# One product of every second block moved from POOL to DVE, and one diagonal of every second pair of groups from POOL to ACT, in a state space layer

## The chip, the cores and the metric

The kernel runs on one core of one Trainium2 chip. The metric is the device time of one execution in microseconds (us). The engines are called PE (matrix products), DVE (vector), ACT (scalar and activation functions), POOL (GpSimd) and SP (which only issues transfers here). SBUF is the memory that all of them work on; PSUM is the small memory into which PE writes.

## The reference

Four layers are applied to x of shape 8 x 512 x 256: three transformer blocks with conditioning, and then a bidirectional state space layer with a gated MLP. Only the last layer is touched. Cut to what matters:

```python
def _mamba(h, ...):                       # h: (8, 512, 256)
    x, z = jnp.split(h @ in_proj_W, 2, axis=-1)        # 512 channels each
    x = silu(causal_conv(x, conv_w) + conv_b)
    xdbl = x @ x_proj_W
    dt = softplus(xdbl[..., :16] @ dt_proj_W + dt_proj_b)
    Bm, Cm = xdbl[..., 16:48], xdbl[..., 48:]          # 32 states
    A = -exp(A_log)
    def step(hst, inp):
        dA = exp(dt_t[:, :, None] * A)
        hst = hst * dA + dt_t[:, :, None] * B_t[:, None, :] * x_t[:, :, None]
        return hst, einsum('bdn,bn->bd', hst, C_t)
    y = scan(step, ...) + Dp * x
    return y * silu(z) @ out_proj_W
...
x = x + g1 * (_mamba(h) + flip(_mamba(flip(h))))       # then norm, gated MLP, residual
```

## The kernel before

The first three layers come first and are left as they are. The state space layer then runs 16 **steps**, one for each of the 8 batch rows b and each direction, forward before reversed. I number them from 0, so even steps are forward and odd steps reversed. All five engines execute in the order in which the program was written (a schedule kept by hand), so an instruction that waits holds up everything behind it on its engine.

A step works on 512 channels in 4 blocks c of 128 and on 32 states in 8 groups of 4, taken as 4 pairs of groups gp. `recur` has 64 iterations k, with c = k // 16, gp = k % 16 // 4 and j = k % 4 (32 channels). For each k:

- `fill` (line 1372): PE multiplies the transposed u times dt (`ut`, one tile per block c) with diagonal matrices `dg` that hold B, and so lays dt * B * x for 128 pairs of channel and state out in PSUM (`bx`, 3 buffers).
- `decay` (line 1347): ACT makes exp(dt * A) in two activations (`da`, `N_DA` = 3 tiles).
- `scan` (line 1386): DVE runs two recurrences of 128 x 512; it is issued two iterations after `fill`. After every second k POOL multiplies four results at once by C (line 1390, `hs` times `cs`).
- `sums` (lines 1411 to 1418): after every four k PE adds over the states into `yc`.

While a step runs, `prep3` prepares the next one. It is a generator that is advanced once for each even k, if the budget `credit` allows: convolution, projections, softplus for `dt`, and last `transposed(c)` for the four blocks. `transposed(c)` first multiplies u by dt into `uc` (line 1132, on POOL), lets two turns pass (`N_UC_LATE`), has PE transpose `uc` in four pieces into a PSUM bank (line 1140) and has ACT copy that to `ut` (line 1145). Block c + 1 starts two turns after block c (`STAGGER`). There is one buffer for `uc` (`N_UC` = 1) and one PSUM bank for all products outside the recurrence; a stream takes it with `free_bank` and gives it up with `taken`. During forward steps from batch row 1 on, the MLP of the batch row before (`project`, `mlp3`) shares that bank: its last products are read by DVE at line 1205. What is left of `prep3` and of the MLP at the end of a step is issued before the next step starts:

```python
            live = [(prep, 0), (post, 1)]
            while any(n == 0 for _, n in live):
```

`diagonal` makes `dg` of the next step for one pair of groups gp and one quarter s of the time axis, in the last block of a step and the beginning of the next:

```python
                    if c == 3 and nxt:
                        for s in range(4):
                            later(1 + 3 * s, lambda gp=gp, s=s: diagonal(nxt, gp, s))
```

A letter for each s says on which engine: "A" is 8 activations of 128 x 64 on ACT (line 1320), "P" is one product of 128 x 512 on POOL and "V" the same on DVE (line 1324). `DIAG` = "AAPA" gives s = 2 to POOL for every gp. The very first pair of groups of step 0 has letters of its own.

Of the kernel before, what the change touches and what calls it, by code (L numbers as in the profile page):

```python
# [10 lines left out]
ALU = mybir.AluOpType  # L11
# [14 lines left out]
N_U, N_UT, N_UC, N_DT, N_HS = 7, 5, 1, 5, 4  # L26
N_DA, AHEAD, SPREAD = 3, 0, (6, 13, 14, 15)
N_UC_LATE = 2
SUMS_LATE, DIAG, STAGGER, RATE, CREDIT = 3, "AAPA", 2, 4.0, 4.0


C_ID, C_MEAN, C_EM, C_E32, C_E64 = 0, 128, 256, 384, 896
# [42 lines left out]
def dit_mamba_kernel(ctx: ExitStack, tc: tile.TileContext, t, out):  # L75
    nc = tc.nc
# [43 lines left out]
    with ExitStack() as actx:  # L120
# [725 lines left out]
        with tc.manual_schedule(  # L846
# [13 lines left out]
            for l, cfg in enumerate(CFGS):  # L860
                us = [u for u in units if u.cfg is cfg]
# [10 lines left out]
    with ExitStack() as mctx:  # L872
# [108 lines left out]
        def free_bank():  # L981

            me = now[0]
            while held[0] or (want[1 - me] and last[0] == me):
                want[me] = True
                yield WAIT
            want[me] = False
            held[0], last[0] = True, me
            return bank()

        def taken():
            held[0] = False
# [26 lines left out]
        def halves(v):  # L1019

            return v.rearrange("p (r s t) -> p s r t", r=2, s=4)
# [36 lines left out]
        def prep3(b, rev):  # L1058
# [16 lines left out]
            us = st.pop("us")  # L1075
# [34 lines left out]
            dt = mp_.tile([128, 4, L], F32, tag="dt", name="dt")  # L1110
# [18 lines left out]
            def transposed(c):  # L1129

                uc = mp_.tile([128, 4, 2, 64], F32, tag="uc", name="uc", bufs=N_UC)
                nc.gpsimd.tensor_tensor(uc, halves(us[c]), halves(dt[:, c, :]), ALU.mult)
                for _ in range(N_UC_LATE):
                    yield 0
                while n_ut[0] - n_ut[1] >= N_UT:
                    yield WAIT
                n_ut[0] += 1
                p = yield from free_bank()
                for s in range(4):
                    nc.tensor.transpose(  # L1140
                        p[:, 128 * s : 128 * s + 128], uc[:, s].rearrange("p r t -> p (r t)"), ident
                    )
                yield 1
                ut = mp_.tile([128, 4, 128], F32, tag="ut", name="ut", bufs=N_UT)
                nc.scalar.copy(ut.rearrange("p s d -> p (s d)"), p)
                taken()
                uts.append(ut)
                yield 0

            live, c, i = [], 0, 0  # L1150
            while live or c < 4:
                if i % STAGGER == 0 and c < 4:
                    live.append(transposed(c))
                    c += 1
                cost = 0
                for g in list(live):
                    n = next(g, None)
                    while n == WAIT:
                        yield WAIT
                        n = next(g, None)  # L1160
                    if n is None:
                        live.remove(g)
                    cost += n or 0
                i += 1
                yield cost + LAST
# [144 lines left out]
        def diagonal(step, gp, s, on=None):  # L1310

            if s == 0:
                dg[step, gp] = mp_.tile([128, 4, 4, 64, 2], F32, tag="dg", name="dg", bufs=n_p)
            o = dg[step, gp][:, s]
            bt = st[("bt",) + step][:, s, 8 * gp : 8 * gp + 8]
            on = on or DIAG[s]
            if on == "A":
                for i in range(2):
                    for n in range(4):
                        nc.scalar.activation(  # L1320
                            o[:, n, :, i], eye, AF.Copy, scale=bt[:, 4 * i + n : 4 * i + n + 1]
                        )
            else:
                (nc.vector if on == "V" else nc.gpsimd).tensor_tensor(
                    o, eye[:, None, :, None].to_broadcast([128, 4, 64, 2]),
                    bt.rearrange("p (i n) -> p n i", i=2)[:, :, None, :].to_broadcast([128, 4, 64, 2]),
                    ALU.mult,
                )
# [22 lines left out]
        def recur(step, nxt, ys):  # L1351
# [75 lines left out]
            for k in range(n_k):  # L1427
                c, gp, j = k // 16, k % 16 // 4, k % 4
                run_due(1)
                if k % 2 == 0:  # L1430
                    fill(k)
                    fill(k + 1)
                    for i in range(0 if k else -AHEAD, 2):
                        decay(step, nxt, k + AHEAD + i)
                n_ut[1] += k % 16 == 15
                later(2, lambda k=k: scan(k))
                if j == 3:
                    later(2 + SUMS_LATE, lambda c=c, gp=gp: sums(c, gp))
# [3 lines that stand above are left out]
                        later(4, lambda gp=gp: spread_c(nxt, gp))  # L1442
                if k % 16 in SPREAD:
                    i = SPREAD.index(k % 16)
                    if c < 3:
                        spread(step, 4 * (c + 1) + i)
                    elif nxt and ("dt",) + nxt in st:
                        spread(nxt, i)
                if not nxt and c == 3 and j == 3 and gp < 3:

                    w = mp_.tile([128, 4, 4, 64, 2], F32, tag="dg", name="dg", bufs=n_p)
                    w = w.rearrange("p s n t i -> p (s n t i)")[:, 0:1024]
                    fetch(("w_g1", "w_g2", "w_g3")[gp], w=w)
                yield k
# [44 lines left out]
        for gp in range(n_p):  # L1499
            spread_c(steps[0], gp)  # L1500
            for s in range(4):
                if gp == 0:
                    diagonal(steps[0], gp, s, "VAVA"[s])
                else:
                    later(4 * gp - 3 + s // 2, lambda gp=gp, s=s: diagonal(steps[0], gp, s))
# [154 lines left out]
```

## Time and profile before

| | |
|---|---|
| Median of 3 runs | 6146.75 us (6141.36 to 6157.84) |
| The profiled execution, its own time | 6153.84 us |
| Span of that profile | 6151.9 us |
| Mean granted TensorE clock | 0.962 |
| Scans, DVE, line 1386 | 2048, mean 1198 ns |
| Products by C, POOL, line 1390 | 512, mean 4569 ns |
| Decays, ACT, line 1347 | 2048, mean 716 ns |
| Fills, PE, line 1372 | 65536 matmuls, 1120.5 us busy |
| Diagonals, ACT, line 1320 | 1528, mean 343 ns |
| Diagonals, POOL, line 1324 | 63, median 1232 ns |
| u times dt, POOL, line 1132 | 64, median 1285 ns |

Times in the profile are microseconds from the start of the span. A row of the timeline reads: start, length, engine, line, operation, tile written and tiles read, shapes, count of merged instructions, and in brackets the idle time before it and what ended it. Instructions of one engine overlap at their ends, so the length of a merged row divided by its count is the pace, and the mean of one is longer. The state space layer takes the span from about 3382 us on.

### The profile page before, as it was taken

The page shows a single profiled execution, that of the slowest core. Times are in us where ns is not written, and L with a number is a line of the kernel's source. Part 1 is how long each engine was busy: PE and PEld are TensorE (multiplying, and loading weights), DVE is VectorE, ACT ScalarE, POOL GpSimd, SP SyncE. Part 2 cuts the span into 40 slices and gives each one's busy share as a digit, 9 for nine tenths or more (in the row PEclk, how much of TensorE's full clock was granted, in tenths as well). Part 3 has the DMA queues.
Part 4 walks back from the last instruction along what each step waited for, and adds up shares of the span by engine and source line. Part 5 has one row for each costly group of instructions (what it writes and reads, how often), then busy time and mean ns, then how long its engine had stood idle before and what let it go on. Part 6 is the DMA issues. An engine that isn't in the chain of part 4 may idle for free. (4 is left out here: it accounts for less than half of the span.)

```text
span 6151.9 us, 221688 instructions
## 1 busy us (share of the span) xinstructions
PE 5588.1 (91%) x99484; PEld 2771.0 (45%) x99484; DVE 4131.2 (67%) x5157; ACT 3556.9 (58%) x6876; POOL 3162.6 (51%) x1419
## 2 busy tenths in 40 slices
PE   8999999999999989899997889898888989888887
PEld 4333334555555543333332445444544545444544
DVE  4554545655656554455541898888888898888987
ACT  2444444444444443344543777777787777777784
POOL 2011002323222231111000899999899999899997
PEclk8999999999999999899998999999999999999999
DMA  2010102332333321110100211222121211222120
GB/s 90 23 27 23 31 22 77 115 89 82 93 88 91 89 79 29 39 27 21 28 14 22 72 55 53 66 58 66 54 67 55 60 55 52 63 61 66 52 67 26
DMA packets 338211, 345.60 MB, mean 56 GB/s; under 512 B 50016, under 2 KB 240480, under 8 KB 337264
## 3 DMA queue, kind: packets, MB, share of 16 engines
q1 hardware_dynamic: 196944, 262.70, 14.8%
q10 hardware_dynamic: 140320, 68.72, 3.9%
q8 instruction: 784, 12.85, 0.9%
q14 instruction: 163, 1.34, 0.1%
HBM read 253.63 MB, written 51.38 MB: 50 GB/s over the span
## 5 line engine op out<-in xcount | busy, mean ns | idle before, releaser
L1386 DVE TENSOR_TENSOR_SCAN hs<-da,bx 128x512 f32<-128x512 f32 x2048 | 2304.4, 1198 | 216.0 <-PE bx L1372 124.2
L1390 POOL TENSOR_TENSOR hs<-hs,cs 128x2048 f32<-128x2048 f32 x512 | 2324.5, 4569 | 216.4 <-DVE hs L1386 139.1
L1347 ACT ACTIVATE da<-dtr,negA 128x512 f32<-128x512 f32 x2048 | 1393.8, 716 | 492.7 <-DVE hs L1386 482.0
L1372 PE MATMUL bx<-dg,ut 64*32 64x128 f32 x65536 | 1120.5, 273 | 194.7 <-DVE hs L1386 100.3
L1372 PEld LDWEIGHTS bx<-dg,ut 64*32 64x32 f32 x65536 | 929.4, 106 | 611.4 <-issue 472.7
L685 DVE TENSOR_REDUCE aux<-s 128x1 f32<-128x512 f32 x1024 | 638.3, 684 | 617.0 <-PE s L680 616.8
L587 POOL TENSOR_SCALAR pr<-pr,sums 128x512 f32<-128x512 f32 x512 | 361.5, 724 | 906.7 <-DVE sums L585 906.7
L736 ACT ACTIVATE pt<-s 128x512 f32<-128x512 f32 x1024 | 528.0, 602 | 468.2 <-PE s L730 467.9
L1418 PE MATMUL yc<-hs,r 128*32 128x512 f32 x4096 | 565.4, 618 | 37.5 <-POOL hs L1390 35.8
L577 ACT ACTIVATE pr<-s,negm 128x512 f32<-128x512 f32 x512 | 345.4, 686 | 249.7 <-DVE negm L576 237.5
L680 PE MATMUL s<-kT,qT 32*128 32x512 f32 x2048 | 374.8, 662 | 63.1 <-ACT pt L736 25.0
L767 PE MATMUL s<-g,w_w 128*128 128x512 f32 x768 | 368.1, 630 | 34.3 <-ACT g L832 34.3
L576 DVE TENSOR_REDUCE negm<-s 128x1 f32<-128x512 f32 x512 | 317.6, 683 | 108.4 <-PE s L566 108.4
L793 POOL COPY aux<-rec 128x1024 f32<-128x1024 f32 x16 | 16.6, 1036 | 718.0 <-DVE rec L791 718.0
L1320 ACT ACTIVATE dg<-eye,bt 128x64 f32<-128x64 f32 x1528 | 381.6, 343 | 0.8 <-PE bx L1372 0.7
L730 PE MATMUL s<-work,kT 32*128 32x512 f32 x2048 | 370.8, 656 | 2.9 <-DVE work L694 2.9
L416 PE MATMUL s<-h,wqkv 128*128 128x512 f32 x768 | 362.3, 611 | 10.1 <-POOL h L403 6.6
L416 PE MATMUL s<-h,w_w 128*128 128x512 f32 x768 | 356.8, 606 | 8.5 <-POOL h L403 8.5
L384 POOL TENSOR_TENSOR xs<-x 128x512 f32<-128x512 f32 x32 | 40.6, 1269 | 622.3 <-DMA x<-x_mid 210.3
L1418 PEld LDWEIGHTS yc<-hs,r 128*32 128x32 f32 x4096 | 120.4, 111 | 384.5 <-issue 268.6
L700 PE MATMUL s<-pt,vt 128*32 128x512 f32 x2048 | 279.9, 617 | 1.3 <-ACT ot L707 1.3
L767 PEld LDWEIGHTS s<-g,w_w 128*128 128x128 f32 x768 | 150.0, 202 | 232.6 <-issue 169.5
(202 smaller groups left out, 6576.8 us busy)
## 6 DMA issues: line engine op xcount, KB each, us to landing
dtr<-dt_s SPq DMA_DIRECT2D x1024, 64.0 KB
qT<-v_dram ACTq DMA_DIRECT2D x256, 128.0 KB
kT<-v_dram ACTq DMA_DIRECT2D x256, 128.0 KB
cs<-c_s SPq DMA_DIRECT2D x256, 128.0 KB
wqkv<-in_wqkv_dram SPq DMA_DIRECT2D x98, 256.0 KB
v_dram<-vt SPq DMA_DIRECT2D x32, 512.0 KB
dt_s<-dt SPq DMA_DIRECT2D x15, 1024.0 KB
x_mid<-x SPq DMA_DIRECT2D x24, 512.0 KB
```

Source lines behind the costliest of these rows:

```text
L416: nc.tensor.matmul(p, w[:, k, o : o + 128], src[:, k, :], start=k == 0, stop=k == n - 1)
L680: nc.tensor.matmul(ss[j], u.qT[r, c, qt * 128 : (qt + 1) * 128], u.kT[r, c, :], start=True, stop=True)
L685: nc.vector.tensor_reduce(negp[c % 2][:, qt, i : i + 1], ss[j], AX.X, ALU.max, negate=True)
L730: nc.tensor.matmul(ss[j], u.kT[r, c, i * 128 : (i + 1) * 128], q2[u, c][r, :], start=True, stop=True)
L736: nc.scalar.activation(pt[j // 2][:, j % 2, :], ss[j], AF.Exp)
L767: nc.tensor.matmul(p, w[:, first + c, m * 128 : (m + 1) * 128], srcs[c], start=c == 0, stop=c == n - 1)
L1320: nc.scalar.activation(o[:, n, :, i], eye, AF.Copy, scale=bt[:, 4 * i + n : 4 * i + n + 1])
L1347: nc.scalar.activation(da[:, i, :], dtr[step, 4 * c + j], AF.Exp, scale=negA[:, 4 * c + j, g : g + 1])
L1372: nc.tensor.matmul(bx[k][32 * n : 32 * n + 32, r, 128 * s : 128 * s + 128], uts[c][64 * r : 64 * r + 64, s, 32 * j : 32 * j + 32], d[64 * ...
L1386: nc.vector.tensor_tensor_scan(h, back(da[:, i, :]), back(x[:, i, :]), 0.0, ALU.mult, ALU.add)
L1390: nc.gpsimd.tensor_tensor(hs[t_], hs[t_], cs[step, k % 16 // 4][:, None, :, :].to_broadcast([128, 2, 2, L]), ALU.mult,)
L1418: nc.tensor.matmul(yc[c][32 * j : 32 * j + 32, :], r32, h[j // 2][:, j % 2, i, :], start=False, stop=gp == n_p - 1 and i == 1, tile_positi ...
```

## The change

In `transposed`, u times dt of blocks 1 and 3 is computed by DVE and that of blocks 0 and 2 by POOL as before. In `diagonal`, the letters depend on gp: for gp 0 and 2 they stay "AAPA", for gp 1 and 3 they are "AAAA".

```diff
-SUMS_LATE, DIAG, STAGGER, RATE, CREDIT = 3, "AAPA", 2, 4.0, 4.0
+SUMS_LATE, DIAG, STAGGER, RATE, CREDIT = 3, ("AAPA", "AAAA"), 2, 4.0, 4.0
...
             def transposed(c):
 
                 uc = mp_.tile([128, 4, 2, 64], F32, tag="uc", name="uc", bufs=N_UC)
-                nc.gpsimd.tensor_tensor(uc, halves(us[c]), halves(dt[:, c, :]), ALU.mult)
+                (nc.vector if c % 2 else nc.gpsimd).tensor_tensor(uc, halves(us[c]), halves(dt[:, c, :]), ALU.mult)
...
             o = dg[step, gp][:, s]
             bt = st[("bt",) + step][:, s, 8 * gp : 8 * gp + 8]
-            on = on or DIAG[s]
+            on = on or DIAG[gp % 2][s]
```

## The prediction

> **What bounds the kernel now.** I read the page's busy shares first, then the waits, then the timeline engine by engine where one step of the state space layer hands over to the next.
>
> ```profile
> PE 5588.1 (91%) x99484; PEld 2771.0 (45%) x99484; DVE 4131.2 (67%) x5157; ACT 3556.9 (58%) x6876; POOL 3162.6 (51%) x1419
> ```
>
> These are averages over four layers. In the window 3570 to 3940 us, inside the state space layer, POOL is busy 344.7 of 370 us, DVE 329.5, PE 326.6 and ACT 291.5, so four engines have little slack and order decides. I call two iterations of k a pair: 4 scans on DVE, 4 decays on ACT, one 4.57 us product on POOL. Inside a step pairs start every 4.44 to 4.5 us and POOL starts 0.2 to 0.5 us behind the scans that feed it: DVE paces POOL there. The excess lies at the handover, which I call a seam. From the start of every 128th scan, steps 2 to 14 last 176.1 us if forward and 167.0 us if reversed, of which one gap of 12.2 us (forward) or 7.5 us (reversed) beyond a normal pair is the seam.
>
> The seam after a reversed step (step 3), PE, POOL and ACT:
>
> ```profile
> 4056.16 0.90 PE L1140 MATMUL bank<-base,uc 128*128 128x128 f32 x4
> 4062.25 1.11 PE L1140 MATMUL bank<-base,uc 128*128 128x128 f32 x4 [5.19 <-POOL uc L1132]
> 4063.29 3.58 PE L1418 MATMUL yc<-hs,r 128*32 128x512 f32 x16
> ...
> 4059.75 1.23 POOL L1324 TENSOR_TENSOR dg<-eye,bt 128x512 f32<-128x512 f32 x1
> 4060.92 1.28 POOL L1132 TENSOR_TENSOR uc<-u,dt 128x512 f32<-128x512 f32 x1
> ...
> 4051.69 2.03 ACT L1320 ACTIVATE dg<-eye,bt 128x64 f32<-128x64 f32 x8
> 4053.61 2.56 ACT L1347 ACTIVATE da<-dtr,negA 128x512 f32<-128x512 f32 x4
> 4056.06 2.02 ACT L1320 ACTIVATE dg<-eye,bt 128x64 f32<-128x64 f32 x8
> 4057.97 0.57 ACT L1145 COPY ut<-bank 128x512 f32<-128x512 f32 x1
> 4063.40 0.59 ACT L1145 COPY ut<-bank 128x512 f32<-128x512 f32 x1 [4.86 <-PE bank L1140]
> ```
>
> PE waits 5.19 us for the fourth product uc, which stands behind POOL's queue. That is what the change attacks, in 7 seams. But ACT has no idle time from 4028.9 to 4058.5, and the copy of the third transpose ends at 4058.5, only 3.7 us before the fourth transpose starts; that transpose needs the one PSUM bank the copy empties.
>
> The seam after a forward step (step 4):
>
> ```profile
> 4223.84 2.02 ACT L1320 ACTIVATE dg<-eye,bt 128x64 f32<-128x64 f32 x8
> 4225.76 2.55 ACT L1347 ACTIVATE da<-dtr,negA 128x512 f32<-128x512 f32 x4
> 4228.21 2.01 ACT L1320 ACTIVATE dg<-eye,bt 128x64 f32<-128x64 f32 x8
> 4230.12 0.56 ACT L1145 COPY ut<-bank 128x512 f32<-128x512 f32 x1
> ...
> 4230.74 4.41 PE L973 MATMUL bank<-g,w 128*128 128x512 f32 x6 [2.49 <-ACT ut L1145]
> ```
>
> Here PE waits not for POOL but for ACT: after the copy, products and transposes go through the one bank in turn until 4241.8, so whatever delays the copy at 4230.12 delays the next step.
>
> **What moves.** 32 of the 64 products uc go from POOL (1.285 us) to DVE. The nearest DVE rows, additions and products of two SBUF tiles of 128x512 (L384, L1324), take 0.69: DVE gains 32 x 0.69 = 22 us. 32 of POOL's 63 diagonals (1.232) become 8 ACT activations each; 16 stand in 3.92 us, so 1.96 per diagonal and 63 us on ACT. POOL loses 32 x 1.285 + 32 x 1.232 = 80.5 us. PE and SP keep their order. None of these totals is the answer; the positions are.
>
> **The new wait.** uc has one buffer. Product c = 1 is now on DVE and may only write once PE has transposed c = 0, and c = 3 once c = 2 is transposed. POOL ran late enough for this to cost little (8.5 us in all). DVE is early: in the built order uc1 stands mid-pair, and DVE reaches it at 4034.65 in step 3 while the transposes of c = 0 end at 4036.53, 1.9 us later (1.9 to 3.4 over the seven reversed steps); uc3 is reached 1.9 to 4.6 us before its transposes end. In forward steps uc1 comes 1.7 to 1.9 us early. Behind a waiting uc stand all scans, and ACT's decays behind those, since three da tiles let ACT run one pair and a half ahead.
>
> Can DVE run uc beside a POOL product? One row bounds it:
>
> ```profile
> 2267.37 2.49 DVE L756 SCALAR_TENSOR_TENSOR x<-y,modT,x 128x512 f32<-128x512 f32 x1 [3.11 <-ACT y L754]
> ...
> 2266.96 2.36 POOL L401 TENSOR_TENSOR h<-h,rstd 128x1024 f32<-128x1024 f32 x1
> ```
>
> The DVE operation, whose large inputs both lie in SBUF, took 2.49 us instead of 0.75 and ended 0.54 us after POOL's at 2269.32. So uc on DVE costs 0.69 if it runs freely and up to 4.57 + 0.69 = 5.26 if it is held from the start of a product. The rows nearest in form give 0.69 and the sum below would be 44; the one row beside a long POOL product gives the remainder of that product and the sum is 52 (reversed seams 1.2 us longer each). I take the second, because POOL is busy 93% of this layer. The Trainium skill, "SBUF — State Buffer", section "Who interferes with whom", has a rule that speaks against this change: a DVE instruction with two SBUF inputs and a GpSimd instruction that reads SBUF exclude each other for the whole instruction, whichever started first, while one SBUF input does not contend. By the rule every uc on DVE pays the remainder and the sum is 52; the scans, one input in PSUM, would stay as they are.
>
> **Reversed seam, walked through** (step 3; half a pair of scans 2.25, a decay pair 1.25, from 4 in 2.55). DVE waits for the transposes until 4036.6; the POOL product begun at 4033.5 ends at 4038.05, so uc1 ends about 4038.65 and every later scan is 4.0 us late. ACT follows: its next decays wait for scans and start at 4040.95, 4043.15, 4045.4 and 4047.65; two diagonals to 4052.7, a pair of decays, the copy of c = 1 to 4055.7, then 16 activations, 8 of them new, to 4059.5, decays to 4062.0, a diagonal to 4064.0, the copy of c = 2 at 4064.45. The fourth transpose starts near 4064.5 instead of 4062.25. uc3 itself, blocked behind a product that ends near 4061.7, is done at 4062.3 and no longer decides. So POOL's wait goes, ACT's copy is late next, and the seam is 2.3 us longer; PE is continuous after it (pairs of 6.4, 5.7, 5.7 us), so this passes on. 7 x 2.3 = 16 us.
>
> **Forward seam** (step 4). POOL's last product ended, a small diagonal is over at 4219.0, so uc1 is not blocked: ready 4219.4, done 4220.05, scans 2.7 late. ACT's decays then wait until 4222.3 and 4224.6; copy of c = 0 ends at 4226.4 instead of 4223.9; 16 activations instead of 8 to 4230.25; decays to 4232.75; diagonal to 4234.7; copy of c = 1 at 4234.7 instead of 4230.1. That is 2.5 from the DVE wait and 2.0 from the new diagonal, 4.5 us, all on the path. uc3 lies between two waits of DVE for PE (4.33 us idle) and is free; were that cover gone it would cost 0.69. 7 x 4.5 = 31.5 us.
>
> **The rest.** The new diagonals for groups 6 and 7 fall three pairs into the next step, beside PE-bound pairs or ACT idle of 1.5 us: nothing, at most 2 us in each of 15 steps if that cover fails. Step 0 starts with ACT continuous from 3392.9 to 3431, and two new diagonals are 3.9 us; I take 3. In step 0 uc1 and uc3 would find their transposes ending 4.1 and 6.6 us later, but POOL lags 3 to 6 us there and absorbs most: 3, between 0 and 12. Before the loop two DVE products replace POOL's in a serial chain: 2 x (1.285 - 0.69) = 1.2 gained. Step 15 makes nothing for a next step.
>
> **Sum:** 16 + 31.5 + 3 + 3 - 1.2 = 52 us. The profiled execution took 6153.84 us (span 6151.9), 7 above the median of the three runs, 6146.75. On the profile that gives 6206, on the median 6199, which I forecast. About 0.3%, 18 us, is what can be told from no change.
>
> **Rivals.** (1) Faster: POOL is the bound and the seam simply loses its wait. Condition: the copy of c = 2 stays at 4058.5, that is, DVE's wait delays no decay and the new diagonal finds a gap. Then the fourth transpose starts at that copy's end, 3.7 us earlier, in seven reversed seams, and forward seams are unchanged: 6147 - 26 = 6121. For it: POOL's 93% and the 5.19 us. Against: ACT without a gap for 30 us. Any gain at these seams ends once the copy slips by 3.7 us. Chance 0.08. (2) Nearly level: only the diagonals count, DVE's waits drown in the seam's idle time. Reversed seams: copy 2.0 late, transpose at 4060.5 instead of 4062.25, 1.7 gained; forward seams 2.0 lost; plus 3: 7 x 0.3 + 3 = 5, so 6152. Against: the decays follow the scans within a pair and a half. 0.13. (3) Much slower: each DVE product meets a fresh POOL product and all of it is on the path: 30 x (0.69 + 4.57 / 2) = 89, so 6236. For it: POOL is hardly ever idle. Against: at forward seams POOL waits for DVE. 0.14. The forecast keeps 0.65.
>
> **Numbers.** Slower by over 0.3% takes the forecast and rival 3, 0.79; within 0.3% rival 2, 0.13; faster rival 1, 0.08. The range runs from rival 2's 6152 to 6240, just past rival 3; the upper end also holds step 0's 12 us and 2 us in each of 15 steps on top of the forecast (6199 + 9 + 30). Left out are rival 1, the lower part of rival 2 and the upper part of rival 3, about 0.2.
>
> **What would show it.** Right: the wait of PE for uc on POOL at the fourth transpose is gone and a wait for ACT's copy stands there; DVE has new waits for L1140; the copy of c = 1 in forward seams lies 4 to 5 us later against the preceding scans; DVE rows of L1132 well over 0.69. Reversed steps lengthen from 167 to 169 us, forward ones from 176 to about 181. Wrong: uc on DVE at 0.69 throughout, or the first scan of a step coming sooner after a reversed step.

## The result, and the profile after

The changed kernel took 6196.55 us, median of six runs (6192.82 to 6214.55), beside 6144.51 us for the kernel before, median of six. The ratio is 1.008, 95% interval 1.0066 to 1.0093, so the change costs 0.8%, 49 us (the two medians differ by 52). The prediction was 6199 us, range 6152 to 6240, slower with a chance of 0.79. The profiled execution's span is 6191.1 us, 39.2 longer than that of before. Single executions of one kernel lie up to 30 us apart here, so times are compared by the ratio and profiles only for where the time lies.

The page's busy row of the changed kernel:

```profile
PE 5594.0 (90%) x99484; PEld 2777.0 (45%) x99484; DVE 4178.8 (67%) x5189; ACT 3618.9 (58%) x7132; POOL 3088.8 (50%) x1355
```

POOL lost 74 us of work and DVE and ACT gained 48 and 62. DVE's 32 products take 50.3 us in all, where 0.69 each would be 22. None of these tells the result. The waits of the layer do (what waited, for whom; total us, times, longest):

```profile
POOL hs L1390 <- DVE hs L1386: 270.2, 131, 14.2
...
DVE uc L1132 <- PE bank L1140: 78.1, 32, 14.1
...
PE bank L1140 <- ACT ut L1145: 36.9, 7, 5.4
```

Before, POOL's wait for the scans was 139.1 us and PE waited 46.8 us for uc on POOL. Now every one of DVE's 32 products waits for PE's transposes, POOL waits twice as long for a DVE that is late, and PE waits for ACT's copy in each of the 7 reversed seams, 5.3 us on average, where it had waited for POOL (5.19 us in step 3).

The reversed seam of step 3 after the change, timeline, DVE, POOL, ACT and PE:

```profile
4046.80 2.01 DVE L1132 TENSOR_TENSOR uc<-u,dt 128x512 f32<-128x512 f32 x1 [1.99 <-PE bank L1140]
4068.59 3.68 DVE L1132 TENSOR_TENSOR uc<-u,dt 128x512 f32<-128x512 f32 x1 [1.99 <-PE bank L1140]
...
4062.66 9.06 POOL L1390 TENSOR_TENSOR hs<-hs,cs 128x2048 f32<-128x2048 f32 x2
...
4051.08 0.72 ACT L1347 ACTIVATE da<-dtr,negA 128x512 f32<-128x512 f32 x1 [0.39 <-DVE hs L1386]
...
4065.12 3.93 ACT L1320 ACTIVATE dg<-eye,bt 128x64 f32<-128x64 f32 x16
4068.95 2.54 ACT L1347 ACTIVATE da<-dtr,negA 128x512 f32<-128x512 f32 x4
4071.40 2.01 ACT L1320 ACTIVATE dg<-eye,bt 128x64 f32<-128x64 f32 x8
4073.31 0.56 ACT L1145 COPY ut<-bank 128x512 f32<-128x512 f32 x1
...
4073.92 1.12 PE L1140 MATMUL bank<-base,uc 128*128 128x128 f32 x4 [5.44 <-ACT ut L1145]
```

Before uc3, DVE waits 1.99 us for the buffer of uc and is then held until POOL's product is over: 3.68 us at 4068.59, and POOL's two products that began at 4062.66 end at 4071.72, so the first 3.1 us are the hold. ACT's decays wait for single scans (0.39 us at 4051.08), then 16 activations stand where there were 8, and the copy of c = 2 ends at 4073.87, just before the fourth transpose. uc itself was ready at 4072.27 and no longer decides.

The forward seam of step 4, ACT and PE, and PE's granted clock in that stretch (in the windows view it is the third figure from the end of the row):

```profile
4233.84 3.94 ACT L1320 ACTIVATE dg<-eye,bt 128x64 f32<-128x64 f32 x16
...
4242.03 0.56 ACT L1145 COPY ut<-bank 128x512 f32<-128x512 f32 x1
...
4242.64 5.49 PE L973 MATMUL bank<-g,w 128*128 128x512 f32 x6 [3.41 <-ACT ut L1145]
...
4250.37 2.84 PE L973 MATMUL bank<-g,w 128*128 128x512 f32 x6 [0.68 <-ACT ut L1145]
```

```profile
4242.60:4248.20 5.60, 5.49 (x6) 1.85 (x6) 0.03 (x1) 0.00 (x0) 2.80 (x1) 0.50 0.22 63
```

PE now waits 3.41 us for the copy of c = 1, 2.49 before, and the six matmuls behind it run at a granted clock of 0.50: 5.49 us, where the same six take 2.84 eight microseconds later.

Step lengths from one profile each (first scan to first scan, us) and the seams, averaged over seven, from the start of the first transpose (c = 0) of the seam:

| | before | after | products alone (E1) | diagonals alone (E2) |
|---|---|---|---|---|
| Step 0 | 158.6 | 167.9 | 160.7 | 165.1 |
| Forward step, mean of 2 to 14 | 176.10 | 180.89 | 175.97 | 178.59 |
| Reversed step, mean of 1 to 13 | 167.03 | 167.37 | 167.25 | 164.74 |
| Forward seam: copy of c = 1 starts | 12.03 | 15.39 | 13.35 | 14.21 |
| Forward seam: PE's products behind it last | 3.71 | 5.10 | 3.33 | 5.07 |
| Forward seam: first scan | 26.62 | 31.61 | 27.80 | 30.15 |
| Reversed seam: copy of c = 2 starts | 22.05 | 27.01 | 25.03 | 23.91 |
| Reversed seam: product uc3 ends | 26.01 | 25.97 | 25.86 | 24.79 |
| Reversed seam: fourth transpose starts | 26.07 | 27.63 | 26.01 | 24.92 |
| Reversed seam: first scan | 31.88 | 33.44 | 32.50 | 30.81 |

Of the 39.2 us between the two spans, 7 x 4.79 = 33.5 lie in forward steps, 7 x 0.34 = 2.4 in reversed ones and 9.3 in step 0; 4.7 are gained before the first scan and 1.4 after step 14. The profiled execution of before ran 9 us above its median and that of after 4 below, so 13 of the 52 us between the medians can't be placed by these two profiles.

### The profile page after: what moved, and what is told of

It is laid out like the page before. It is cut to its first block, busy times and chain, and to the rows that moved or that the text cites. A ratio compares the mean times of both kernels' runs of the same rounds, so it can differ in the third digit from the quotient of the medians.

```text
span 6191.1 us, 221887 instructions
## 1 busy us (share of the span) xinstructions
PE 5594.0 (90%) x99484; PEld 2777.0 (45%) x99484; DVE 4178.8 (67%) x5189; ACT 3618.9 (58%) x7132; POOL 3088.8 (50%) x1355
## 4 chain that ended last, share of the span: by engine, by line
PE 68%; ACT 11%; DVE 9%; issue 5%; POOL 4%; DMA 1%; SPq 1%; ACTq 0%; POOLq 0%; DVEq 0%
PE s L416 11%; PE bx L1372 9%; PE s L767 9%; DVE hs L1386 8%; PE s L730 5%; PE s L680 5%; PE yc L1418 5%; PE s L612 5%; PE bank L973 4%; PE s L700 4%; PE s L566 3%; ACT dg L1320 3%; ACT da L1347 3%; POOL hs L1390 3%; PE bank L1046 3%
## 5 line engine op out<-in xcount | busy, mean ns | idle before, releaser
L1320 ACT ACTIVATE dg<-eye,bt 128x64 f32<-128x64 f32 x1784 | 442.5, 342 | 1.1 <-PE bx L1372 1.0
L680 PEld LDWEIGHTS s<-kT,qT 32*128 32x128 f32 x2048 | 108.7, 188 | 324.9 <-issue 106.4
```

The costliest lines, as they stand in the source:

```text
L680: nc.tensor.matmul(ss[j], u.qT[r, c, qt * 128 : (qt + 1) * 128], u.kT[r, c, :], start=True, stop=True)
L1320: nc.scalar.activation(o[:, n, :, i], eye, AF.Copy, scale=bt[:, 4 * i + n : 4 * i + n + 1])
```

## The experiments

The theory: at each seam a chain of waits through single buffers decides. DVE's product waits for the one uc buffer and for POOL's product; scans, decays and ACT's copies queue behind it; the new diagonals lengthen ACT's queue ahead of the same copies. The main rival: ACT's extra diagonals do it alone.

### E1 and E2: one half of the change each

E1 is the kernel before with the products of blocks 1 and 3 on DVE; E2 is the kernel after with all products on POOL:

```diff
 # E2, against after
-                (nc.vector if c % 2 else nc.gpsimd).tensor_tensor(uc, halves(us[c]), halves(dt[:, c, :]), ALU.mult)
+                nc.gpsimd.tensor_tensor(uc, halves(us[c]), halves(dt[:, c, :]), ALU.mult)
```

> Only the first half of the change: u times dt of blocks 1 and 3 on DVE, the diagonals as before. Theory (a chain at the seams: DVE waits for the transposes and for POOL's product, ACT's decays wait for DVE, ACT's copy of the transposed block comes late, and the next transpose or product needs the PSUM bank that the copy empties): forward seams 2.8 us longer, reversed seams about level, since uc3 on DVE ends about when POOL's did, step 0 4 us longer, 1.2 us gained before the loop: 20 us slower than before. Rival, the diagonals alone do it: level or up to 5 us faster. Rival, DVE's own time alone does it: the whole of the measured 50 us.

> Only the second half: all diagonals of every second pair of groups on ACT, u times dt wholly on POOL. Theory: forward seams 2.0 to 2.5 us longer by one diagonal ahead of ACT's copy, reversed seams about 1 us shorter, because POOL loses one diagonal ahead of the fourth product and ACT's copy still ends before it, step 0 5 us longer: 12 us slower than before. Rival, the diagonals alone do it: 50 us slower. Rival, DVE alone: level.

Measured: E1 1.0005 (0.9997 to 1.0014), that is 3 us slower or level; E2 1.0036 (1.0024 to 1.0048), 22 us. Both were expected otherwise, and they add up to 25 us where the whole change costs 49. Fourth transposes of step 3, E1 first and then E2:

```profile
4060.17 1.09 PE L1140 MATMUL bank<-base,uc 128*128 128x128 f32 x4 [3.84 <-DVE uc L1132]
```

```profile
4066.81 1.12 PE L1140 MATMUL bank<-base,uc 128*128 128x128 f32 x4 [4.59 <-POOL uc L1132]
```

In both halves the product still decides, not the copy. The table shows why: a fourth transpose starts at the later of two events, the end of uc3 and the end of the copy of c = 2 (its start + 0.56). Before, the copy had 26.01 - 22.61 = 3.4 us to spare. DVE's waits delay it by 3.0, the new diagonal by 1.9: each alone stays inside, both together (5.0) overrun it by 1.6. E2 even gains 1.1 there, as POOL makes one diagonal fewer ahead of uc3. Halves against whole, 1.56 - (-0.06) - (-1.15) = 2.8 us in each of 7 seams is 19 of the 24 us that the halves leave unexplained (14 if the first scan is taken in place of the fourth transpose). In forward seams the halves do add up (1.18 + 3.53 against 4.99). Whole forward steps do not: -0.13 and 2.49 in the halves against 4.79, another 2.4 us in each of 7 steps, because the forward steps of E1 and E2 are 1.0 to 1.3 us shorter than before ahead of the seam. Why is open; the seven forward steps of before alone scatter from 173.8 to 177.3. So the overrun is shown as a cause of the shortfall, not as all of it.

The main rival gets a part of the time. By the ratios the products cost 3 us if they are moved first and 27 if last (the whole less E2), the diagonals 22 or 46. Where the late product on POOL hides them in reversed seams (E2), the diagonals cost least.

### E3, E4 and E7: a second buffer for uc

```diff
-N_U, N_UT, N_UC, N_DT, N_HS = 7, 5, 1, 5, 4
+N_U, N_UT, N_UC, N_DT, N_HS = 7, 5, 2, 5, 4
```

E3 is this in the kernel after, E4 in E1, E7 in the kernel before.

> The whole change with two buffers for uc, so that a product on DVE need not wait for the transposes of the block before. Theory: in forward seams DVE no longer waits 1.8 us, so ACT's copy is late by the diagonal and about 1 us only: 1.6 us per forward seam back, 11 us; in reversed seams and in step 0 the product on DVE then meets the running POOL product earlier and waits for its end all the same, so little changes: 35 to 40 us slower than before instead of 50. Rival, the wait for the transposes is all of DVE's share and POOL holds up nothing: 15 us slower than before.

> u times dt of blocks 1 and 3 on DVE with two buffers, the diagonals as before. Theory, with what the first four runs showed: in reversed seams the copy of block 2 is still 3 us late, because uc1 on DVE still waits for POOL's running product, and the fourth transpose comes only 0.4 us sooner; forward seams 0.5 us longer: level, within 5 us of before. Rival, the wait for the transposes was DVE's whole share: the fourth transpose 2 to 3 us sooner in seven seams, 15 to 20 us faster.

> The kernel before with two buffers for uc and nothing else. Theory: uc stays behind POOL's queue, so PE's wait of 5.2 us for the fourth product in reversed seams stays; POOL's own waits for the buffer were 8.5 us in all: level, at most 5 us faster. Rival, the one buffer is what holds the seams: 20 us or more faster.

Measured: E3 1.0062 (1.0049 to 1.0075), 38 us slower, as expected; E4 0.9983 (0.9974 to 0.9992), 10 us faster, a miss, since level within 5 was expected; E7 0.9993 (0.9985 to 1.0002), level as expected. E4's fourth transpose starts at 25.94, hardly sooner than before, so where its gain comes from is open. The buffer by itself is worth nothing that can be told from noise, and in the changed kernel it gives back only about 11 of 49 us (the intervals of E3 and of the whole change just overlap), although DVE's wait is gone. E3's first product of step 3's seam on DVE, and POOL:

```profile
4041.16 4.08 DVE L1132 TENSOR_TENSOR uc<-u,dt 128x512 f32<-128x512 f32 x1
```

```profile
4035.58 9.11 POOL L1390 TENSOR_TENSOR hs<-hs,cs 128x2048 f32<-128x2048 f32 x2
```

The bracket with the wait is gone, but the instruction lasts 4.08 us, as long as wait and hold together had (1.99 + 2.01). DVE now arrives about a microsecond into a POOL product and is held until it ends, at 4044.69. Two barriers stood one behind the other with nearly the same end; taking one away leaves the other.

### E5: a product with one SBUF input

In the kernel after, blocks 1 and 3 are made on DVE by a reduction over an axis of length 1, which reads u alone (dt is left out of these blocks, here and in the same lines of E12 and E13):

```diff
+                if c % 2:
+                    nc.vector.tensor_reduce(uc, halves(us[c])[:, :, :, :, None], AX.X, ALU.add)
+                else:
+                    nc.gpsimd.tensor_tensor(uc, halves(us[c]), halves(dt[:, c, :]), ALU.mult)
```

> The whole change, but blocks 1 and 3 are made on DVE by an operation with one SBUF input of the same size (a reduction over an axis of length 1), which leaves out the factor dt in these two blocks. It still waits for the transposes. Theory: if two SBUF inputs are what POOL holds up, each of these 32 operations takes about 0.7 us, also beside POOL's product, and the 1.3 and 3 us that the reversed seams show per operation vanish; since ACT's copy and not uc3 decides there, only about 1.3 us per reversed seam comes back: 40 us slower than before. Rival, any DVE operation at this place is held up: durations up to 3.7 us remain and the time stays at 50 us slower. Rival, the port decides all of it: 30 us come back.

Measured: 1.0069 (1.0057 to 1.0081), 42 us slower, as expected. All uses of the tile uc by DVE, count, then shortest, median and longest in ns, in E5 and in the kernel after:

```profile
L1133 DVE TENSOR_REDUCE uc<-u x32: 685/686/687, 3388.2 to 5993.8; 128x512 f32<-128x512 f32 x32
```

```profile
L1132 DVE TENSOR_TENSOR uc<-u,dt x32: 691/700/3684, 3381.3 to 5993.8; 128x512 f32<-128x512 f32 x32
```

With one SBUF input none of the 32 is held, though 17 of them run beside a POOL product. A reduction is also another operation than a product, but the scans have two inputs as well, one of them (`bx`) in PSUM, and none of them is held beside POOL's products either, in the kernel after:

```profile
L1386 DVE TENSOR_TENSOR_SCAN hs<-da,bx x2048: 1185/1195/1222, 3396.6 to 6147.0; 128x512 f32<-128x512 f32 x187
```

So the hold goes with the second input in SBUF. Its price in the changed kernel is small, about 7 us by the ratios, whose intervals overlap: the wait for the buffer is still there, the other barrier again.

### E8, E10 and E12: only block 3 on DVE

If E4 gains, one product on DVE, the one that PE waits for, might gain more. E8 is the kernel before with two buffers and

```diff
+                (nc.vector if c == 3 else nc.gpsimd).tensor_tensor(uc, halves(us[c]), halves(dt[:, c, :]), ALU.mult)
```

> Only block 3 on DVE, two buffers for uc, the diagonals as before: the one product that PE waited for moves, the one that delays ACT's decays (block 1) stays on POOL. Theory: the copy of block 2 stays where it was in reversed seams, so the fourth transpose starts behind it, 2.5 to 3.5 us sooner, PE idles shorter and its next sums run faster; forward seams level; step 0 up to 2 us longer: 15 to 25 us faster than before. Rival, a DVE operation beside POOL costs as much as it brings: level.

Measured: 0.9979 (0.9969 to 0.9989), 13 us faster, a little less than expected. Step 3, DVE, POOL and PE:

```profile
4053.65 7.69 DVE L1132 TENSOR_TENSOR uc<-u,dt 128x512 f32<-128x512 f32 x1
...
4050.58 9.04 POOL L1390 TENSOR_TENSOR hs<-hs,cs 128x2048 f32<-128x2048 f32 x2
4059.59 1.20 POOL L1324 TENSOR_TENSOR dg<-eye,bt 128x512 f32<-128x512 f32 x1
...
4061.49 1.09 PE L1140 MATMUL bank<-base,uc 128*128 128x128 f32 x4 [5.39 <-DVE uc L1132]
```

DVE's product is held not for one POOL instruction but for the rest of a product, a whole second product and a diagonal, and ends 0.55 us after POOL's queue has run dry at 4060.79. E12 puts E5's reduction in place of that one product:

> As the run with block 3 alone on DVE and two buffers, but block 3 is made by the operation with one SBUF input, which leaves out the factor dt in that block. In the run with two inputs the operation took up to 7.7 us, until POOL had ended two products and a diagonal that ran without a gap. Theory: that hold needs the second SBUF input; here the operation takes 0.69 us, the fourth transpose starts at 22.6 us after the first instead of 25.7, and 15 to 25 us are gained on the run with two inputs. Rival, DVE reaches the place late for another reason: no more than 3 us of difference.

Measured: 0.9935 (0.9923 to 0.9947), 27 us faster than E8 by the difference of the ratios, a little more than expected. In step 3 the reduction runs freely beside POOL's products, DVE and POOL:

```profile
4041.10 0.66 DVE L1133 TENSOR_REDUCE uc<-u 128x512 f32<-128x512 f32 x1
...
4038.02 9.07 POOL L1393 TENSOR_TENSOR hs<-hs,cs 128x2048 f32<-128x2048 f32 x2
```

The fourth transpose of the reversed seams starts at 22.64 instead of 25.66 and the first scan at 27.92 instead of 32.12. The hold was what ate E8's gain.

E10 is E8 with one of ACT's diagonals (s = 1 of gp 1 in reversed steps) given to POOL, to free ACT ahead of the forward seam's copies:

```diff
+            on = on or ("P" if step[1] and gp == 1 and s == 1 else DIAG[s])
```

> The run with only block 3 on DVE, and besides one diagonal more on POOL instead of ACT, that of the second pair of groups and the second quarter, when the next step is a reversed one: the opposite of the change at the place where ACT's copy decides. Theory: in forward seams the copy of block 1 comes 2 us sooner and PE's product behind it runs faster after a shorter idle time, 2.0 to 2.7 us in seven seams: 15 us faster still than the run with block 3 alone, 30 to 40 us faster than before. Rival, POOL is the bound and pays for one more product: 5 to 10 us slower than that run.

Measured: 0.9985 (0.9975 to 0.9994), a miss: no better than E8. The copy of c = 1 in forward seams starts at 11.25 against 12.05, 0.8 us sooner and not the 2 us of a diagonal. Step 4, PE:

```profile
4218.09 2.84 PE L973 MATMUL bank<-g,w 128*128 128x512 f32 x6 [2.10 <-ACT ut L1145]
4222.17 0.66 PE L1140 MATMUL bank<-base,uc 128*128 128x128 f32 x4 [1.25 <-POOL uc L1132]
4223.50 4.54 PE L973 MATMUL bank<-g,w 128*128 128x512 f32 x6 [0.67 <-ACT ut L1145]
```

Here PE's first products are quick (in three of the seven forward seams, as in E8), but PE then waits 1.25 us for the product uc of c = 2 on POOL, whose queue holds the extra diagonal, and it is the second products that run slowly (4.54 for 2.84).

### E11, E13 and E14: PE's fourth transpose waits for no product

E11 leaves the change out and lets POOL begin the last block one turn earlier, with two buffers. It is the whole computation:

```diff
-                if i % STAGGER == 0 and c < 4:
+                if c < 4 and i >= (0, 2, 4, 5)[c]:
```

> No DVE product at all: all four products stay on POOL, with two buffers, and block 3 starts one turn after block 2 instead of two, so that its product stands one POOL product of 4.57 us earlier in POOL's queue; the diagonals as before. Theory: in reversed seams the fourth product ends near 21.5 us after the first transpose instead of 26.0, so the fourth transpose starts behind ACT's copy at 22.6 instead of 26.1: 2.5 to 4 us in seven seams, forward seams level: 15 to 30 us faster than before, 10 to 25 faster than the second buffer alone. Rival, POOL's total work is what counts and its order does not: level with the second buffer alone.

Measured: 6115.71 us, 0.9945 (0.9933 to 0.9958), 34 us faster than the kernel before, a little more than expected, and the quickest complete version of all. The fourth transposes of step 3:

```profile
4041.58 0.75 PE L1140 MATMUL bank<-base,uc 128*128 128x128 f32 x4 [2.41 <-ACT ut L1145]
```

PE's wait for POOL, which the change set out to shorten, is gone by order and a second buffer, without another engine. The buffer alone (E7) leaves the fourth transpose at 26.27; the order without the buffer was not run. PE waits 2.41 us for ACT's copy instead of 5.19 for POOL, and the fourth transpose of the reversed seams starts at 22.85 instead of 26.07.

E13 is the kernel after with two buffers and E5's reduction, so that DVE has neither wait nor hold. E14 is E11 with the change's diagonals. (Its expectation says that blocks 2 and 3 start earlier. As in E11 only block 3 does: in step 3 of E11 its product starts 19.4 us after the first transpose, 25.0 before, and that of block 2 at 13.6 in both.)

> The whole change with two buffers and with the operation with one SBUF input for blocks 1 and 3, which leaves out the factor dt there: DVE does the same amount of work at the same places but waits neither for the transposes nor for POOL. Theory: what is left is the share of the diagonals, as in the run with the diagonals alone: 15 to 25 us slower than before. Rival, DVE's added work and its place in the queue cost by themselves: 40 to 50 us slower.

> All products uc stay on POOL with two buffers, blocks 2 and 3 are started one and two turns earlier (as in the version that was about 34 us faster than before), and the diagonals of gp 1 and 3 are all on ACT as in the change. It prices the diagonals where PE waits for no uc at a seam. By the prediction's price, 2.0 us of ACT on the path in 7 forward and 7 reversed seams and 3 in step 0, they cost 31 us and the kernel is level with before, within 5. By the seams measured since (copy of c = 1 about 2.2 later and PE's product after it 1.2 slower in forward seams, 1.7 in reversed ones, 6 in step 0) they cost about 40 us and it is 5 to 10 slower than before. If ACT absorbs the diagonals once POOL is out of the way, it stays 34 faster.

Measured: E13 1.0013 (1.0003 to 1.0022), 8 us slower, less than expected, since reversed seams are 1.56 us shorter than before (first scan at 30.32) while forward ones stay 3.24 longer. With both barriers gone the changed kernel costs 41 us less than it did, where either barrier alone had given 11 and 7. E14 1.0012 (1.0002 to 1.0023), 7 us slower, so the diagonals take back all that E11 gained: 0.0067 x 6147 = 41 us, between 27 and 55 by the ends of the two intervals. The 40 read from the seams is nearer than the prediction's 31, but both lie inside, and by their profiles steps 0 to 14 of the two kernels differ by 24 us only. A forward seam of E14:

```profile
4226.95 4.72 PE L973 MATMUL bank<-g,w 128*128 128x512 f32 x6 [5.08 <-ACT ut L1145]
```

PE waits twice as long for the copy as before (2.49 in the prediction's row), and the products behind it last 4.72 us. From E11 to E14 the copy of c = 1 is 2.09 later and PE's products behind it last 4.77 instead of 3.78: 3.1 us per forward seam, two thirds of it the diagonal itself.

In all fourteen kernels, seam by seam, the fourth transpose of the reversed seams starts within 0.2 us of the later of the two events. The averages of eight of them:

| | copy of c = 2 ends | uc3 ends | fourth transpose |
|---|---|---|---|
| before | 22.61 | 26.01 | 26.07 |
| E1 | 25.59 | 25.86 | 26.01 |
| E2 | 24.47 | 24.79 | 24.92 |
| after | 27.57 | 25.97 | 27.63 |
| E11 | 22.70 | 20.24 | 22.85 |
| E12 | 22.58 | 18.56 | 22.64 |
| E13 | 24.32 | 17.52 | 24.38 |
| E14 | 24.55 | 20.34 | 24.70 |

## Why the prediction was right

**The direction and the mechanism.** The signs it named are there: PE's wait at the fourth transpose is for ACT's copy, DVE waits for line 1140, DVE's rows of line 1132 are well over 0.69 in places, forward steps last 180.9 us (about 181 predicted). Two are weaker than named: the forward copy of c = 1 is 3.4 us later instead of 4 to 5 (counted here from the first transpose), and reversed steps last 167.4 instead of 169. The holds come out as walked: uc1 was to end 2.05 us after its wait and took 2.01, and uc3 in step 3 did run beside POOL's product until that ended (3.68). Rival 1, a plain gain, needed the copy of c = 2 to slip by less than 3.7 us; it slipped by 5.0. Rival 2, that only the diagonals count, gave 5 us for them; alone they cost 22 (E2), and the whole costs twice that. Rival 3, a fresh POOL product each time, fails on the median of 700 ns: half of DVE's products run free.

**Forward seam, 4.5 us each: right sum, wrong terms.** Measured 4.79 per step and 4.99 to the first scan. The prediction put all of it on the copy of c = 1, 2.5 for DVE's wait and 2.0 for the diagonal. The copy moved by 3.36 (1.32 in E1, 2.18 in E2). The rest is PE's products behind the copy, 3.71 to 5.10 us at the lower clock, which no step of the prediction held. DVE's wait was priced too high and the clock at nothing; that the two errors cancel is luck. How much of the slower products belongs to the change is not settled: over the seven seams they last 4.57 to 5.10 us in the six kernels with the change's diagonals and 2.84 to 4.05 in seven of the eight without, but 4.87 in E7, whose copy starts at 12.12, nearly as before.

**Reversed seam, 2.3 us each: 1.6 measured, and 0.34 in the step.** The copy of c = 2 was walked to 5.95 us later and came 5.0 later. One reason is in the rows: the walk let ACT wait for pairs of scans, while each decay follows a single scan (the row at 4051.08 and its like). Further, the first 25 pairs of reversed steps became 1.07 us shorter (125.15 against 126.22), which gives back most of the seam. That shortening is also there in E12 (125.12) and E7 (125.10), where POOL has all its diagonals, and of all fourteen profiles that of before has the longest such stretch; its cause stays open. By whole steps, then, reversed ones brought 2.4 us of the 16 predicted.

**Step 0, 6 us: 9.3 measured.** Its first five pairs took 3.05 longer (3 predicted), the waits of uc 4.0 (3 predicted, between 0 and 12), and pairs 30 and 31 at its end another 1.9, which was not foreseen.

**Before the loop, 1.2 us gained:** from the first product to the first scan 17.85 us against 19.07, 1.2. The other 3.4 of the earlier first scan lie ahead of the first product and are not the change.

**The sum.** 52 predicted, 49 measured by the ratio, 52 by the medians. So close a sum is partly luck, as its terms were off by more: 16 for reversed seams against 11 by the seams or 2.4 by the steps, 6 for step 0 against 9.3. The weighing of hold against free run (52 or 44) was right in kind: the holds exist, and E5 puts them at about 7 us against the 8 taken. The Trainium skill, "SBUF — State Buffer", section "Who interferes with whom", says that a DVE instruction with at most one SBUF input, outside the 2-port perf modes, does not contend with GpSimd; E5's flat 685 to 687 ns agrees.

**What the prediction did not see** is that its terms are not additive. It walked the whole change, which saved it. Priced half by half, as its expectations for E1 and E2 then did, it was wrong both times.

## What to carry to other kernels

Where a step waits for the later of two chains, cost the whole change along both chains at once: halves that cost 3 and 22 us alone cost 49 together here, and of two barriers with nearly the same end either gave 11 or 7 us when it was taken away alone, and both together 41. Before moving work off a queue because something waits for it, ask whether it can stand earlier in the same queue: one line of order and a second buffer gained 34 us here, where the move of the products to another engine was level alone and the whole change lost 49. An engine with time to spare is no free place for an instruction that has to wait, if everything behind it must wait too (E8 against E12, 27 us).

## What the hardware showed

A DVE instruction with two SBUF inputs that meets a running POOL instruction is not always let in when that one ends. In E8 it was held through a following product and a diagonal in six of the seven reversed seams (7.67 to 7.70 us). In E1, where a product was followed at once by a diagonal, DVE went in between and POOL's instruction was stretched instead:

```profile
4059.41 1.69 POOL L1324 TENSOR_TENSOR dg<-eye,bt 128x512 f32<-128x512 f32 x1
```

Alone that diagonal takes 1.2 us. What decides between the two was not found.

In the rows shown, PE's products behind a wait of 2.49 to 5.08 us lasted 4.41 to 5.49 us where the same six matmuls take 2.84 elsewhere; the granted clock was 0.50 for the longest. In other seams they took 2.84 behind waits of up to 3.17 us (E12). The Trainium skill, "TensorE: Matmul & The Clock Gate", section "What's actually happening", gives a half clock after an idle window of about 3.4 us; here the wait before the 5.49 us was 3.41, but a wait of 2.49 already went with 0.64 (the products at 4230.74 before the change), and one of 5.08 with 0.60 (E14). The length of the wait alone does not give the loss; in the mean of seven seams of one profile each the products lasted 1.4 us longer after the change.
